# A four-layer graph and feed-forward kernel: making the feed-forward weights in the first stage, spreading the last close over the first slots, and adding the last constant by DMA

## The chip, the cores and the metric

The kernel runs on one core of one Trainium2 chip. The metric is the device time of one launch in microseconds; the time before is the median of three runs. A profile is of one further execution on the chip.

## The reference, cut to what matters

Two layers work on x (4096 rows of 256 columns) and on a sparse integer matrix adj (4096 by 4096). Layer 0 is a graph attention and a feed-forward loop, layer 1 two chained graph attentions and a mixture of experts. Each adds to x.

```python
# layer 0
h = einsum('nd,mdo->mno', layernorm(x), W)                 # 4 heads of 64
e = leaky_relu(f_src[:, :, None] + f_dst[:, None, :], 0.2) # f = h . a1, h . a2
x = x + elu(softmax(where(adj > 0, e, -9e15)) @ h)         # heads side by side
y = layernorm(x)
for _ in range(30):                                        # the feed-forward loop
    y = y + 0.01 * tanh(y)
    y = y * sigmoid(y)
    y = layernorm(y, ln_w, ln_b) @ W_ffn.T + b
x = x + y
# layer 1
x = x + gat(gat(layernorm(x)))      # two attentions as above
x = x + experts(layernorm(x))       # router, top 2 of 6, three matmuls each
```

## The kernel before, in words

One core runs five stages one after the other: attention g0, the feed-forward loop, attentions g1 and g2, the experts. Rows come in 32 tiles of 128; a group is 4 tiles (512 rows), so there are 8 groups. DRAM buffers lie between stages: x1d after g0, x2d after the feed-forward, h1d and x3d after g1 and g2.

**An attention stage** (`attention`) has a first part, its preparation, and a main loop. The preparation goes over the 8 groups: it transposes rows on PE, multiplies them by the head weights, and writes `vals`, two fp16 parts of every value. Small matmuls of all kinds share one PSUM tile there, `small_ps`. In g0 the weights of g0, g1 and g2 are made in it too (list `late`), and the mask pieces are begun: adj comes in 64 loads of 1 MB (`load_piece`, two buffers), VectorE makes a byte pair of each (`make_piece`, L214), a DMA transposes it.

The main loop has 128 units: 4 chunks of 8 row tiles, by 4 heads, by 8 slices q of the columns. Per unit, ScalarE and VectorE make sign tiles `st` (L461, L459), VectorE ANDs the mask in (L567) and XORs the rest (`below`, L573), and PE does 64 fp8 by fp16 matmuls into the accumulators `acc` (L519). After eight units a head is closed: ScalarE scales the low half out of PSUM (`lower_sums`, L468, tile `lo`), VectorE adds (`whole_sums`, L472, tile `u`), which frees the accumulators, and the generator `close` does the rest one step per unit: scale by r, add, add hs, reciprocal and scale, exp into tile `e` (L497), and `finish`, which makes `e` the result (L622, L623) and stores it by the SP queue (L624). `u`, `e` and `old` have one buffer each, `lo` has two. A manual schedule keeps the program's order on VectorE and ScalarE in this loop; the other queues, SP's among them, are ordered by the framework's scheduler. The last head is closed after the loop, all at once.

**The feed-forward stage** first loads its weight by the ScalarE queue, normalizes and scales it through a chain of small operations on PE, VectorE and POOL (L703 to L772), and measures the first groups of x1d. Then it runs 240 slots (30 steps by 8 groups) and six more to drain. A slot issues work of several ages, `slot(at)`:

```python
u = at - 3   # PE transposes z; at end ScalarE copies zT (L846), POOL makes z_rs (L850, L851)
u = at - 5   # VectorE: y = po * rstd + bias, or + last in the last step (L803)
u = at - 2   # ScalarE silu (L815), fp16 parts (L817, L818), SP transposes them (L822)
u = at       # ScalarE tanh (L826), POOL adds (L827); VectorE statistics of u = at - 2
rate(at + 2); init(at + 1); measure(at + 3)   # only in the first eight slots
u = at - 4   # PE: 20 matmuls (L863, L866)
u = at - 5   # last step only: POOL adds y to x1 (L877), SP stores x2d (L878)
```

`measure` takes statistics of a group of x1d on VectorE (L676, L678), `rate` makes the factor and shift x_rs and x_nm on ScalarE and POOL (L684 to L688), `init` applies them on ScalarE into y (L695). All four engines keep the program's order here. The rows of the last four groups of x1d that the end adds are loaded into own tiles (L790), the other four by the stream of row tiles (L92).

Of the kernel before, what the change touches and what calls it, by code (L numbers as in the profile page):

```python
# [11 lines left out]
F32 = mybir.dt.float32  # L12
BF16 = mybir.dt.bfloat16
F16 = mybir.dt.float16
# [32 lines left out]
def gnn_ffn_kernel(ctx: ExitStack, tc: tile.TileContext, a: dict, out: bass.AP):  # L47
# [19 lines left out]
    ones = const.tile([2 * H, P], F32, name="ones")  # L67
    nc.gpsimd.memset(ones, 1.0)
# [10 lines left out]
    x1d = dram.tile([N, C], F32, name="x1d")  # L79
    x2d = dram.tile([N, C], F32, name="x2d")  # L80
# [7 lines left out]
    stream = []  # L88

    def load_ahead(src, g, view=rows_of, queue=nc.sync):  # L90
        t = stream[-1].tile([P, G, C], F32, name="rows")
        queue.dma_start(t, view(src, g))  # L92
        ahead[g] = t

# [32 lines left out]
    def weights(tag, W, a_src, a_dst, norm):  # L127
# [4 lines left out]
        def load(pool):  # L132
            for k in range(KC):
                nc.scalar.dma_start(
                    w[:, k, :C].rearrange("p (h o) -> p h o", h=H),
                    W[:, k * P : (k + 1) * P, :].rearrange("h p o -> p h o"),
                )
            ab = pool.tile([P, 2, H, D], F32, name=f"{tag}_ab")
            nc.scalar.dma_start(ab[:, 0], bcast_rows(a_src))
            nc.scalar.dma_start(ab[:, 1], bcast_rows(a_dst))  # L140
            return ab

        def make(pool, small_ps, ab):
            prod = pool.tile([P, 2, H, D], F32, name="prod")
# [16 lines left out]
    def attention(tag, src, norm, w, others, chunks, first, ends, following):  # L161
# [7 lines left out]
        with ExitStack() as scope:  # L169
            lay = scope.enter_context(tc.tile_pool(name=f"{tag}_lay", bufs=1))  # L170
            vals = lay.tile([P, NT, H, 2, 2, DV], F16, name="vals")
            r = lay.tile([P, NT, H], F32, name="r")
            nf2 = lay.tile([P, NT, H], F32, name="nf2")
            hs = lay.tile([P, 1, H, DV], F32, name="hs")
            mask = [scope.enter_context(tc.tile_pool(name=f"{tag}_mask", bufs=4))]
# [20 lines left out]
            def load_piece(n):  # L196
# [3 lines left out]
                arow[n] = stream[-1].tile([P, 2, 8 * P], I32, name="adj")  # L200
# [32 lines left out]
            with ExitStack() as ps:  # L233
# [44 lines left out]
                def greatest():  # L278
# [8 lines left out]
                    nc.vector.tensor_scalar(dm, ident[: 2 * H, : 2 * H], fx, None, op0=OP.mult)  # L287
                    pt = small_ps()
                    nc.tensor.matmul(pt[:, : 2 * H], ones, dm, start=True, stop=True)
# [107 lines left out]
                late = [functools.partial(make, prep, small_ps, get(prep)) for get, make in others]  # L397
                for g in range(NG + 2):
# [19 lines left out]
                    if g in (3, 5) and late:  # L418
                        late.pop(0)()
                nc.vector.tensor_tensor(r, fs[:, :, :H], mb.to_broadcast([P, NT, H]), OP.add)  # L420
# [17 lines left out]
            end = scope.enter_context(tc.tile_pool(name=f"{tag}_end", bufs=1))  # L438
# [37 lines left out]
            def close(c, h, u):  # L476
# [19 lines left out]
                e = end.tile([P, CM, D], F32, name="e")  # L496
# [40 lines left out]
            with tc.manual_schedule(engines={mybir.EngineType.DVE, mybir.EngineType.Activation}):  # L537
# [3 lines left out]
                for at in range(len(units) + LAG):  # L541
# [43 lines left out]
                    if first:  # L585
# [8 lines left out]
                        if at == len(units) - 30:  # L594
                            store_mask(len(chunks) * PER // 4 - 1)
                    if following and at == len(units) - 2 * following[0]:
# [6 lines left out]
            for _ in close(c, h, u):  # L603
                pass

    def to_rows(dst, src=None):
# [5 lines left out]
        def begin(t, n, h, work):  # L612
            if src is not None:
                old = work.tile([P, 8, D], F32, name="old")
# [20 lines left out]
    with tc.tile_pool(name="adj", bufs=2) as adjacency:  # L635
        stream.append(adjacency)
        attention("g0", x, True, w0, [make, *makers], [8, 8, 8, 8], True, to_rows(x1d, x), [])
    stream.append(ctx.enter_context(tc.tile_pool(name="stream", bufs=4)))

    with ExitStack() as scope:
        one = scope.enter_context(tc.tile_pool(name="f_one", bufs=1))
        wT = one.tile([P, C], F32, name="wT")  # L650
        w16 = one.tile([P, 2, C], F16, name="w16")
        scale = one.tile([P, 2], F32, name="scale")
        under = one.tile([P, 2, G], F32, name="under")
        eps = one.tile([P, 2], F32, name="eps")
        nc.gpsimd.memset(eps[:, :1], EPS)
        nc.gpsimd.memset(eps[:, 1:], EPS * 1e-4)
        bias = one.tile([P, C], F32, name="bias")
        last = one.tile([P, C], F32, name="last")
# [4 lines left out]
        x1 = {}  # L663

        def load(g, queue=nc.sync):
            if g not in ahead:
                load_ahead(x1d, g, queue=queue)
            x1[g] = ahead.pop(g)

        measured, rates = {}, {}  # L670

        def measure(g):
            st = small.tile([P, G, 6], F32, name="x_st")
            mv = measured[g] = small.tile([P, G, 2], F32, name="x_mv")
            for r in range(G):
                nc.vector.bn_stats(st[:, r, :], x1[g][:, r, :])  # L676
            for r in range(G):
                nc.vector.bn_aggr(mv[:, r, :], st[:, r, :])  # L678

        def rate(g):  # L680

            mv = measured.pop(g)
            rs = small.tile([P, G], F32, name="x_rs")
            nc.scalar.activation(rs, mv[:, :, 1], AF.Identity, scale=1e-4, bias=eps[:, 1:])  # L684
            nc.gpsimd.tensor_tensor(rs, rs, mhalf, OP.pow)
            nm = small.tile([P, G], F32, name="x_nm")
            nc.gpsimd.tensor_tensor(nm, mv[:, :, 0], rs, OP.mult)
            nc.gpsimd.tensor_scalar(nm, nm, -1.0, None, op0=OP.mult)  # L688
            rates[g] = rs, nm

        def init(g):
            t = x1.pop(g)
            rs, nm = rates.pop(g)
            for r in range(G):
                nc.scalar.activation(  # L695
                    y[:, g * G + r, :], t[:, r, :], AF.Identity, scale=rs[:, r : r + 1], bias=nm[:, r : r + 1]
                )

        for g in range(4):
            load(g, nc.gpsimd)  # L700
        with tc.tile_pool(name="f_prep", bufs=1) as prep, tc.tile_pool(name="f_pps", bufs=1, space=PSUM) as pps:
            ln = prep.tile([2 * KC, P], F32, name="ln")
            nc.scalar.dma_start(ln[:KC], a["L0_ffn_ln_w"].rearrange("(k p) -> k p", p=P))  # L703
            nc.scalar.dma_start(ln[KC:], a["L0_ffn_ln_b"].rearrange("(k p) -> k p", p=P))
            wr = prep.tile([P, KC, C], F32, name="wr")
            nc.scalar.dma_start(wr, a["L0_ffn_W"].rearrange("(k p) c -> p k c", p=P))
            nc.scalar.dma_start(bias, bcast_rows(a["L0_ffn_b"]))
            for g in range(3):
                measure(g)
                if g < 2:  # L710
                    rate(g)
            init(0)
            ps = pps.tile([P, 2 * KC], F32, name="ps_ln")
            nc.tensor.transpose(ps, ln, ident[: 2 * KC, : 2 * KC])
            lnT = prep.tile([P, 2 * KC], F32, name="lnT")
            nc.vector.tensor_scalar(lnT, ps, 100.0, None, op0=OP.mult)
            lbb = prep.tile([P, KC, P], F32, name="lbb")
            nc.vector.tensor_copy(lbb, lnT[:, KC:, None].to_broadcast([P, KC, P]))
# [661 lines left out]
```

## Time and profile before

| | |
|---|---|
| median of 3 runs | 3016.61 us (3013.63 to 3020.14) |
| the profiled execution, own time | 3008.46 us |
| its span | 3006.8 us |
| mean granted TensorE clock | 0.974 |
| g0, preparation, to its first L519 matmul | 0 to 95.6 us |
| g0, main loop, to its last L519 matmul | 95.6 to 598.4 us |
| first tanh of the feed-forward; its POOL sum in slot 8 | 608.6 us; 652.4 us |
| last tanh of the feed-forward; last POOL sum into x2d | 1553.4 us; 1583.4 us |
| first L519 matmul of g1 | 1644.3 us |

A line of a timeline reads: start in microseconds from the span's start, length, engine, source line, operation, tile written and tiles read, sizes, count, and in brackets the idle time before it and what ended it. `SPq` and `ACTq` are DMAs issued by those queues; the length is then that of the issue. A DMA's landing is not in that line; it is taken from the trace's records of landings, at the sixteenth and last of its parts.

### The profile page before, as it was taken

What the parts mean: (1) busy time and instruction counts of PE and PEld (TensorE: products, weight loads), DVE (VectorE), ACT (ScalarE), POOL (GpSimd) and SP (SyncE); (2) the same over time, 40 slices, a digit from 0 to 9 for tenths busy, and PEclk for the clock granted to TensorE, in tenths of its full rate; (3) what the DMA queues carried; (4) which work ended last, traced back from release to release, by engine and by line L of the source; (5) the groups of instructions that cost most, each with busy time, mean ns of one, the idle gap of its engine ahead of it and who ended that gap; (6) DMA issues with size and microseconds to landing.
All of it is one profiled execution on the core that took longest, in us unless ns stands there. A gap on an engine that the chain in (4) does not pass through costs nothing. (4 is left out here: it accounts for less than half of the span.)

```text
span 3006.8 us, 82646 instructions
## 1 busy us (share of the span) xinstructions
PE 2813.1 (94%) x33923; PEld 2568.3 (85%) x33923; DVE 2741.0 (91%) x5766; ACT 2462.0 (82%) x3132; POOL 1173.2 (39%) x1056
## 2 busy tenths in 40 slices
PE   6899999979999999999998999999889999986996
PEld 5799999958888888888876999999789999975996
DVE  8999999989999999999998899999689999986775
ACT  5799999788888888888866999999699999963442
POOL 2000000089999999999993000000200000013663
PEclk9999999989999999999999999999999999997998
DMA  9999784143333333333343031220303132133253
GB/s 292 267 256 249 224 247 118 33 133 70 68 68 67 68 70 69 68 68 68 68 95 121 20 103 51 76 79 27 107 20 93 51 107 79 51 96 123 82 172 134
DMA packets 482899, 320.08 MB, mean 106 GB/s; under 512 B 416573, under 2 KB 443354, under 8 KB 476378
## 3 DMA queue, kind: packets, MB, share of 16 engines
q1 hardware_dynamic: 467698, 287.13, 35.6%
q0 software_dynamic: 7680, 21.51, 2.3%
q10 hardware_dynamic: 7144, 6.16, 0.6%
q8 instruction: 268, 4.39, 0.6%
q14 instruction: 109, 0.89, 0.1%
HBM read 183.00 MB, written 52.04 MB: 78 GB/s over the span
## 5 line engine op out<-in xcount | busy, mean ns | idle before, releaser
L519 PE MATMUL acc<-vals,st 128*128 128x130 f16 x12288 | 1431.1, 218 | 36.1 <-DVE u L472 27.9
L519 PE MATMUL acc<-vals,below 128*128 128x130 f16 x12288 | 1430.7, 221 | 12.6 <-DVE below L573 11.9
L461 ACT ACTIVATE st<-f1b,nf 128x1024 int8<-128x1024 f32 x1265 | 1334.2, 1142 | 29.9 <-PE acc L519 24.6
L519 PEld LDWEIGHTS <-below 128*128 128x128 fp8e4 x12288 | 1175.7, 96 | 49.4 <-issue 44.5
L519 PEld LDWEIGHTS <-st 128*128 128x128 fp8e4 x12288 | 1207.5, 98 | 9.6 <-DVE st L567 7.5
L863 PE MATMUL po<-wT,zT 128*128 128x256 f32 x1920 | 576.1, 382 | 7.4 <-ACT zT L846 7.4
L827 POOL TENSOR_TENSOR th<-th,y 128x1024 f32<-128x1024 f32 x240 | 568.2, 2368 | 27.2 <-ACT th L826 4.4
L866 PE MATMUL po<-w,zT 128*128 128x256 f16 x3840 | 577.9, 273 | 0.3 <-DMA zT<-z 0.3
L866 PEld LDWEIGHTS <-zT 128*128 128x128 f16 x3840 | 376.3, 98 | 161.6 <-DMA zT<-z 1.2
L573 DVE TENSOR_TENSOR below<-m,st 128x1024 int32<-128x1024 int32 x384 | 470.0, 1224 | 32.8 <-DVE st L567 1.3
L567 DVE TENSOR_TENSOR st<-st,m 128x1024 int32<-128x1024 int32 x384 | 467.5, 1217 | 0.2
L803 DVE SCALAR_TENSOR_TENSOR y<-po,z_rs,bias 128x256 f32<-128x256 f32 x928 | 384.4, 477 | 2.1 <-PE tp L796 0.7
L839 DVE BATCH_NORM_STATS2 z_st<-z 128x6 f32<-128x256 f32 x960 | 335.8, 413 | 0.0
L863 PEld LDWEIGHTS po<-wT,zT 128*128 128x128 f32 x1920 | 291.1, 192 | 17.4 <-ACT zT L846 9.0
L105 POOL TENSOR_TENSOR ln_rstd<-ln_rstd,mhalf 128x4 f32<-128x4 f32 x24 | 32.3, 1345 | 586.5 <-ACT acc L1033 491.8
L815 ACT ACTIVATE z<-th 128x1024 f32<-128x1024 f32 x240 | 251.2, 1047 | 8.6 <-POOL th L827 8.3
L826 ACT ACTIVATE th<-y 128x1024 f32<-128x1024 f32 x240 | 249.8, 1041 | 0.1
L850 POOL TENSOR_TENSOR z_rs<-z_rs,mhalf 128x4 f32<-128x4 f32 x240 | 245.7, 1024 | 0.0
L846 ACT COPY zT<-tp 128x512 f32<-128x512 f32 x240 | 140.4, 585 | 110.5 <-PE tp L796 110.4
L459 DVE TENSOR_SCALAR st<-f1b,nf 128x1024 int8<-128x1024 f32 x271 | 201.2, 743 | 8.4 <-PE acc L519 8.4
L436 POOL MEMSET hs<- 128x4 f32 x3 | 0.3, 101 | 491.9 <-DVE u L489 491.9
L818 DVE SCALAR_TENSOR_TENSOR z<-z,scale,z 128x512 f16<-128x512 f32 x240 | 179.4, 747 | 4.9 <-ACT z L817 4.9
(252 smaller groups left out, 2970.2 us busy)
## 6 DMA issues: line engine op xcount, KB each, us to landing
adj<-in_adj_dram SPq DMA_DIRECT2D x64, 1024.0 KB
m<-edges SPq DMA_DIRECT2D x32, 1024.0 KB
f1b<-fd SPq DMA_DIRECT2D x48, 512.0 KB
edges<-m SPq DMA_DIRECT2D x16, 1024.0 KB
y<-yd SPq DMA_DIRECT2D x16, 512.0 KB
ew<-in_L_ffn_expert_w_dram SPq DMA_DIRECT2D x18, 256.0 KB
t<-in_x_dram SPq DMA_DIRECT2D x8, 512.0 KB
old<-in_x_dram SPq DMA_DIRECT2D x16, 256.0 KB
```

Source lines behind the costliest of these rows:

```text
L461: nc.scalar.activation(out, f1, AF.Sign, bias=f2, scale=-1.0)
L519: nc.tensor.matmul(acc[:, i, cols], masked[part][:, at_i // TR, s, rows], v[:, cols], start=(j == 0 and part == 0), stop=(j == NT - 1 and ...
L567: nc.vector.tensor_tensor(above, above, whole, OP.bitwise_and)
L573: nc.vector.tensor_tensor(below, whole, above, OP.bitwise_xor)
L803: nc.vector.scalar_tensor_tensor(y[:, g * G + r, :], po[:, r, :], rstd[:, r : r + 1], last if end else bias, op0=OP.mult, op1=OP.add,)
L815: nc.scalar.activation(z, th.pop(u), AF.Silu, scale=0.01)
L826: nc.scalar.activation(th[at], y[:, g * G : (g + 1) * G, :], AF.Tanh, scale=0.01)
L827: ins = nc.gpsimd.tensor_tensor(th[at], th[at], y[:, g * G : (g + 1) * G, :], OP.add)
L839: nc.vector.bn_stats(st[:, r, :], z[:, r, :])
L850: nc.gpsimd.tensor_tensor(rs[u], rs[u], mhalf, OP.pow)
L863: nc.tensor.matmul(po[:, r, :], src[:, r * P : (r + 1) * P], wT, start=True, stop=False)
L866: nc.tensor.matmul(po[:, r, :], src16[:, part * G + r, :], w16[:, other, :], start=False, stop=(part == 1 and other == 1),)
```

## The change

Each part is in the diff below, which is cut to what the prediction speaks of.

- The feed-forward weight is loaded and made in g0's preparation (`load_ffn`, `make_ffn`, fourth of the list `late`, at g == 7). Some steps go from VectorE to ScalarE or POOL.
- One persistent `ring` of four row tiles replaces the two adj buffers and the stream of row tiles; `e` becomes the other half of `u`; `old` shares the two buffers of `lo`; the preparation's temporary tiles lie in `u` and `lo` (`spots`). This holds for all three attentions.
- In g0's last 28 units, `side` issues the loads of four groups of x1d, six `add_last`, two `measure`, two `rate` and two `init`. `add_last(g)` copies a group of x1d to x1e in DRAM by SP and adds `last` to it by an accumulating DMA of POOL, for groups 0 to 5.
- The last close of g0 becomes the generator `outro`: its first step follows the loop, the others are in slots 0, 2 and 3. Groups 6 and 7 are loaded after it.
- In the first eight slots `init(at)` stands ahead of the tanh of the same slot, `rate(at + 1)` behind POOL's sum, and both work in place on the loaded rows.
- In the last step, groups 0 to 5 add x1e on VectorE (`po * rstd + x1e`) and need no POOL sum; groups 6 and 7 keep it, now right behind VectorE's.
- In the experts, `numbers` makes its long table in four parts.

```diff
-    def load_ahead(src, g, view=rows_of, queue=nc.sync):
-        t = stream[-1].tile([P, G, C], F32, name="rows")
+    ring = keep.tile([P, 4, G, C], F32, name="ring")
+    def load_ahead(src, g, view=rows_of, queue=nc.sync):
+        t = ring[:, turns[0] % 4]
...
-                arow[n] = stream[-1].tile([P, 2, 8 * P], I32, name="adj")
+                arow[n] = ring[:, 2 * (n % 2) : 2 * (n % 2) + 2].rearrange("p s r c -> p s (r c)").bitcast(I32)
...
-                e = end.tile([P, CM, D], F32, name="e")
+                e = u[:, :, 1, :D]
...
-                old = work.tile([P, 8, D], F32, name="old")
+                old = work.tile([P, 4, 2, DV], F32, name="old", tag="lo", bufs=2)
...
-                    if g in (3, 5) and late:
+                    if g in (3, 5, 7) and late:
                         late.pop(0)()
...
+                    if len(units) - at in side:
+                        side[len(units) - at]()
...
-            for _ in close(c, h, u):
+            closing = close(c, h, u)
+            if tail is not None:
+                next(closing)
+                return closing
+            for _ in closing:
                 pass
...
+    def add_last(g):
+        ins = nc.sync.dma_start(rows_of(x1e, g), rows_of(x1d, g))
+        tc.add_manual_dep(ins.ins, arrived[0].ins.name,
...
+        nc.gpsimd.dma_start(rows_of(x1e, g), last[:, None, :].to_broadcast([P, G, C]), accum_op=OP.add)
...
+    SUMMED = 6
+    side = {
+        28: [(load, g) for g in range(4)],
+        **{24 - 3 * g: [(add_last, g)] for g in range(SUMMED)},
+        8: [(measure, 0)],
+        5: [(measure, 1)],
+        4: [(rate, 0)],
+        2: [(rate, 1)],
+        1: [(init, 0), (init, 1)],
+    }
...
+                t = x1.pop(g) if end else None
+                summed = end and g < SUMMED
                 for r in range(G):
                     nc.vector.scalar_tensor_tensor(
-                        y[:, g * G + r, :],
+                        t[:, r, :] if summed else y[:, g * G + r, :],
                         po[:, r, :],
                         rstd[:, r : r + 1],
-                        last if end else bias,
+                        t[:, r, :] if summed else last if end else bias,
...
+                if end and not summed:
+                    nc.gpsimd.tensor_tensor(t, t, y[:, g * G : (g + 1) * G, :], OP.add)
+                if end:
+                    nc.sync.dma_start(rows_of(x2d, g), t)
...
-                nc.scalar.activation(th[at], y[:, g * G : (g + 1) * G, :], AF.Tanh, scale=0.01)
+                if 2 <= at < NG:
+                    init(at)
+                was = x1.pop(at) if at < NG else y[:, g * G : (g + 1) * G, :]
+                nc.scalar.activation(th[at], was, AF.Tanh, scale=0.01)
...
-            if at + 2 < NG:
-                rate(at + 2)
-            if at + 1 < NG:
-                init(at + 1)
-            if at + 3 < NG:
-                measure(at + 3)
+            if 2 <= at + 1 < NG:
+                rate(at + 1)
+            if at == 0:
+                next(outro)
+                measure(3)
+            if at == 2:
+                next(outro)
...
+            if at == 3:
+                for _ in outro:
+                    pass
+                for g in range(SUMMED, NG):
+                    load_apart(x1d, g)
+            if 4 <= at + 2 < NG:
+                measure(at + 2)
...
-            u = at - 5
-            if units - NG <= u < units:
-                g = u % NG
-                t = x1.pop(g)
-                nc.gpsimd.tensor_tensor(t, t, y[:, g * G : (g + 1) * G, :], OP.add)
-                nc.sync.dma_start(rows_of(x2d, g), t)
```

## The prediction

> **What bounds the kernel now.** I read the page's busy times first, then the stretches by stage, then the timelines of the three places that the change touches: the head boundaries of the attentions, the first slots of the feed-forward and its last ones.
>
> ```profile
> PE 2813.1 (94%) x33923; PEld 2568.3 (85%) x33923; DVE 2741.0 (91%) x5766; ACT 2462.0 (82%) x3132; POOL 1173.2 (39%) x1056
> ```
>
> PE and VectorE are both nearly full over the span, so there is little free cover on VectorE. The stretches (busy time and count of PE, weight loads, VectorE, ScalarE, POOL) are g0's main loop, the feed-forward's start, its steady part:
>
> ```profile
> 95.60:598.20 502.60, 480.21 (x8192) 475.28 (x8192) 483.52 (x532) 475.16 (x479) 3.77 (x4) 0.99 0.71 197
> 598.20:652.40 54.20, 31.04 (x162) 22.09 (x160) 44.03 (x145) 44.42 (x78) 38.98 (x46) 0.75 0.55 158
> 652.40:1553.40 901.00, 901.00 (x6439) 737.87 (x6437) 898.86 (x2992) 783.58 (x1154) 863.04 (x691) 1.00 0.35 68
> ```
>
> In the main loop a unit takes 3.69 us of PE, and the loss is at head boundaries: in chunks 0 to 2 PE waits 0.7 to 3.2 us ahead of a head's first matmul, in chunk 3, g1 and g2 0.5 us in its middle. What ends it is the sum that frees the accumulators. From the list of who waited for L472, in us and times:
>
> ```profile
>   PE acc L519: 27.9, 45
> ```
>
> The feed-forward's start has all engines part idle: 54 us for what becomes 3.9 us a slot. Between slots 3 and 7 the tanh comes every 5.47 us, and POOL is what is full. Slot 4 of the POOL timeline:
>
> ```profile
> 632.56 2.37 POOL L827 TENSOR_TENSOR th<-th,y 128x1024 f32<-128x1024 f32 x1
> 634.88 1.04 POOL L850 TENSOR_TENSOR z_rs<-z_rs,mhalf 128x4 f32<-128x4 f32 x1
> 636.00 0.20 POOL L851 TENSOR_TENSOR z_rs<-z_rs,under 128x4 f32<-128x4 f32 x1
> 636.15 1.01 POOL L685 TENSOR_TENSOR x_rs<-x_rs,mhalf 128x4 f32<-128x4 f32 x1
> 637.24 0.51 POOL L687 TENSOR_TENSOR x_nm<-x_mv,x_rs 128x4 f32<-128x4 f32 x1
> 637.84 0.23 POOL L688 TENSOR_SCALAR x_nm<-x_nm 128x4 f32<-128x4 f32 x1
> 638.03 2.36 POOL L827 TENSOR_TENSOR th<-th,y 128x1024 f32<-128x1024 f32 x1
> ```
>
> From one th sum to the next POOL never rests; x_nm is ready 5.5 us after the sum began. ScalarE's init, which uses such an x_nm one slot later, and tanh:
>
> ```profile
> 633.14 2.06 ACT L695 ACTIVATE y<-rows,x_nm,x_rs 128x256 f32<-128x256 f32 x4
> ...
> 636.82 1.04 ACT L826 ACTIVATE th<-y 128x1024 f32<-128x1024 f32 x1
> ```
>
> At the end, POOL's sums into x1 push its th sums apart, 6.3 us where 3.92 is the pace:
>
> ```profile
> 1553.00 2.37 POOL L877 TENSOR_TENSOR rows<-rows,y 128x1024 f32<-128x1024 f32 x1
> 1555.33 2.35 POOL L827 TENSOR_TENSOR th<-th,y 128x1024 f32<-128x1024 f32 x1
> ...
> 1559.33 2.37 POOL L877 TENSOR_TENSOR rows<-rows,y 128x1024 f32<-128x1024 f32 x1
> 1561.65 2.80 POOL L827 TENSOR_TENSOR th<-th,y 128x1024 f32<-128x1024 f32 x1
> ```
>
> [...] The trace agrees where DMA is quiet (g1's head stores land 2.55 us after issue) and shows up to 5.2 where it is not. [...] the one at 616.23 shows 1.28 us and no drain, so I use 1.28. [...] a VectorE multiply of 128x1 took 2.29 us (616.10) beside POOL's sum; L687 varies from 0.19 to 0.62.
>
> **The change part by part.**
>
> (a) *Weight in g0's preparation.* From 28 us on VectorE is back to back there, and it sets when the main loop begins. It gains (rows of 602 to 621 us) lnT 0.15, bias 0.42, two subtractions 0.75, two reductions 0.83, nine small ones at some 0.12, wT 0.38, w16's second part 0.45: 4.0 us. In the built order the last of these stand between the sign tiles and the first `below`, and wait for POOL's power (0.58) and ScalarE's w16 (0.35); pieces and values of the last group stand around the earlier waits. I add 0.5: **+4.5** (2 to 6.5; the low end if VectorE's gaps, 0.2 to 0.5 us each, take half). The loads go by ScalarE's queue at 0.25 to 0.5 us an issue, beside work. The first stage's PE and ScalarE additions lie in their gaps. Moving the weight frees nothing at 602 to 621 by itself; that is counted in (e).
>
> (b) *e in u.* New wait: the first sum of a head (L472) writes u, so it must wait for the store of the head before, which reads u. In the built order this sum now has a DMA semaphore among its waits, at all 45 boundaries; before, it waited for ScalarE alone. SP and VectorE at one boundary:
>
> ```profile
> 563.64 0.36 SPq L624 DMA_DIRECT2D x1d<-e  x1
> ```
>
> ```profile
> 567.32 0.69 DVE L472 TENSOR_TENSOR u<-acc,lo 128x520 f32<-128x520 f32 x1
> ```
>
> The sum starts 3.68 us after the store's issue, the store lands 4.86 after it: 1.18 us short. The same subtraction at every boundary gives, where positive, in g0's chunks 0 to 2 0.92, 1.61, 0.45, 0.01, 0.46, 0.29, around chunk 3 0.07, 0.82, 1.18, in g1 1.39, 0.74, 1.33, 0.74, in g2 1.05, 0.72, 1.44. Behind that sum stand VectorE's AND and XOR, and PE waits for the accumulators. In chunks 0 to 2 PE already waits for exactly this, so it adds in full: 3.7. Elsewhere the present stall of 0.5 takes the first half microsecond: 0.3 + 2.2 + 1.7 (the 1.18 goes under (d)). Sum **+8** (2 to 14: the high end adds all shortfalls in full and something for the wait itself).
>
> (c) *Copies and accumulating DMAs.* SP isn't under the manual order. In the built order the copies of groups 0 and 1 stand ahead of the store of the head before last of chunk 2, and wait for the first load of x1d; those of 4 and 5 wait for the next store. So at the boundary into chunk 3, two 512 KB copies are in front of a store that had 4.2 us. No DRAM-to-DRAM copy is in the trace; a 512 KB load lands in 3.7 to 4.5 us[...]. POOL's six accumulating DMAs run beside it; POOL itself is idle (4 instructions in the loop). I take **+4** (0 to 7) at this one boundary.
>
> (d) *measure in the last units.* Two of 1.73 us (1.37 + 0.36) go into VectorE's order at 8 and 5 units from the end, where VectorE's `below` is 0.8 to 2.0 us ahead of PE. The first delays a head's sum by 1.7, less the present 0.5: 1.2; with the third measure spread over the last units the lead is used up, 1.3 more: **+2.5** (0.5 to 4). init of two groups, 4.1 us, falls into ScalarE's idle 8.6 us at 588 to 596: nothing.
>
> (e) *First slots.* Keep the last matmul at 598.4. ScalarE has lo by 599.1 and goes to tanh at once: POOL's first th sum at 600.2, not 609.7, and slot 2 no longer waits for the weight. But init(at) now stands ahead of tanh(at), and rate(at + 1) behind the th sum of slot at on POOL. That closes a ring: th sum, z_rs, rate on POOL 5.5 us, then init 2.06, tanh 1.04 and two hand-overs of 0.07, then the next th sum: 8.75 us a slot, where 5.47 was. Step by step, slot 2 sums at 609.9; exp between two silus costs two more table loads (2.6), so slot 3 sums at 618.2; then 626.95, 635.7, 644.45, 653.2, and slot 8 at 656.95 (3.75 later). Before, slot 8 summed at 652.4. So 9.5 us early becomes **+4.5** late (1 to 7: L687 at its 0.2 or 0.6 in each turn[...]). What is late next is y of slot 5, which waits for nothing else.
>
> (f) *Last slots.* Six of eight POOL sums of 2.36 go, and SP no longer holds transposes behind x2d stores that wait for POOL. At a pace of 3.92 from 1546.75 the last y begins at 1574 and ends at 1575.3, not 1581.7; PE is free at 1573.5, not 1579.2. g1's preparation follows PE and these rows: **-6** (-8 to -4).
>
> The ring, `lo` for `old`, and the split table (iotas and casts of POOL, some 4 us at 2694 to 2699, read from 2727 on) I cost at nothing: the rows' buffers alternate as before, and 28 us cover the table. Without that cover the table costs at most 2.
>
> Sum: 4.5 + 8 + 4 + 2.5 + 4.5 - 6 = **+17.5**, on the profiled execution's 3008.46. That one lies 8.2 under the median; against 3016.6 I forecast **3034**.
>
> **Rivals.** *Faster*, 0.11: POOL does rate in the shadow of ScalarE and the ring of (e) does not bind. Then slots 4 to 8 keep 5.47, (e) is -8.5, and with (a), (b) and (c) at their low ends, 2, 2 and 0, the sum is -8: 3009. It decides at a turn under some 6.5 us. For it: the work is the same and two inits fewer. Against: POOL's program order. *No change*, 0.12: stores land in time, (b) and (c) vanish into existing stalls; 4.5 + 2.5 + 4.5 - 6 = 5.5, 3022, or less. For it: g1's quiet landings of 2.55. *Worse*, 0.14: the copies and accumulating DMAs slow all of chunk 3's stores by 3 us or more, and (b) reaches its high end: +31, 3048. That the change doesn't do what it says is not among them: the built order shows each piece in place.
>
> **How the numbers follow.** The forecast has 0.63. About 0.2% (6 us) is what a measurement of this kernel can tell from no change. Slower holds the forecast and the worse case, 0.77; the same 0.12; faster 0.11. The parts' ends, half of each added in squares, give about 9 us either way for the forecast; to leave no more than 2 in 10 out with the no-change and worse cases, the range is 3012 to 3047.
>
> **What would show it.** In the changed profile: L472's successor idle for a DMA of x1d, h1d and x3d; PE's first L519 near 100; the boundary into chunk 3 worst; tanh of slots 4 to 7 some 8.7 us apart; th sums evenly 3.92 apart to the end. Tanh steps of 5.5, or a u sum that starts as early as before, would make it wrong.

## The result, and the profile after

The changed kernel has a median of 3028.91 us (3026.85 to 3038.2); the kernel before, run beside it, 3018.47 (3013.63 to 3026.25). The ratio is 1.0038 [1.0026, 1.005], some 11.5 us more. In a later comparison it was 1.0026 [1.0016, 1.0037]. The kernel before takes 3006 to 3024 us from one chip to another, so only ratios to runs beside it are compared. The two profiled executions are 21 us apart (own times 3008.46 and 3029.54), more than the medians: that pair misleads, and the table takes each kernel twice.

| stretch, us | before, two profiles | after, two profiles | difference of means | predicted |
|---|---|---|---|---|
| start to first matmul of the main loop | 95.6, 95.1 | 103.2, 103.5 | +8.0 | +4.5 (a) |
| g0's main loop | 502.8, 506.1 | 509.1, 510.7 | +5.5 | +10.5 (b, c, d) |
| its end to the th sum of slot 8 | 54.0, 54.0 | 59.4, 59.5 | +5.5 | +4.5 (e) |
| slots 8 to 200 | 751.8, 751.8 | 752.2, 753.6 | +1.1 | 0 |
| slots 200 to 239 | 157.5, 157.5 | 153.0, 153.0 | -4.5 | with the next |
| last th sum to g1's first matmul | 82.7, 81.5 | 77.4, 77.6 | -4.6 | -6 with the one above (f) |
| g1's main loop | 486.8, 485.6 | 488.0, 487.9 | +1.8 | +2.2 (b) |
| g2's preparation | 64.9, 65.2 | 54.3, 53.2 | -11.3 | 0 |
| g2's main loop | 485.7, 486.4 | 488.8, 490.1 | +3.4 | +1.7 (b) |
| last stage | 325.1, 323.0 | 342.5, 326.6 | not repeated | 0 |

The last stage's code differs in the table of `numbers` and in where its rows lie. Rows one to nine add up to +4.9; the forecast had +17.5 for them, and the -11.3 not at all. The last stage's 342.5 did not come back in the second profile. Between +4.9 and the measured 7.8 to 11.5 lie 3 to 7 us that the last stage and the spread between executions may hold; they are not settled.

The page's busy times after:

```profile
PE 2812.7 (93%) x33923; PEld 2566.3 (85%) x33923; DVE 2733.1 (90%) x5756; ACT 2467.5 (81%) x3139; POOL 1177.9 (39%) x1061
```

No engine's work changed by more than 8 us over the span: what was added is mostly waiting. The stretches of g0's main loop, the feed-forward's first slots and its steady part (busy time and count of PE, weight loads, VectorE, ScalarE, POOL; then the PE clock, DMA share and GB/s):

```profile
103.20:612.10 508.90, 483.00 (x8192) 477.98 (x8192) 484.44 (x537) 480.28 (x490) 17.65 (x14) 0.99 0.77 207
612.10:671.70 59.60, 27.13 (x145) 19.56 (x143) 36.93 (x121) 43.34 (x69) 35.70 (x38) 0.77 0.44 115
671.70:1572.90 901.20, 901.06 (x6437) 737.68 (x6436) 898.88 (x2991) 783.29 (x1154) 863.48 (x691) 1.00 0.39 69
```

In the first slots there is less to do, since the weight is made elsewhere, and yet more idle time: VectorE is busy for 37 of 59.6 us, where it was for 44 of 54.2. The loop grew with its PE work unchanged. Who ended VectorE's idle time ahead of the sum into u (us, times), and how long PE waited for that sum:

```profile
  DMA h1d<-u: 11.0, 4
  DMA x1d<-u: 5.7, 3
  DMA x3d<-u: 5.5, 3
...
  PE acc L534: 35.1, 46
```

The stores of x1d, h1d and x3d now hold the sum up, as (b) said, and PE's wait for it went from 27.9 to 35.1. (The last line is of the list of who waited for the sum.) In the first slots, slot 5 on POOL, then the ScalarE steps of slot 6:

```profile
651.20 2.35 POOL L894 TENSOR_TENSOR th<-th,x 128x1024 f32<-128x1024 f32 x1 [3.28 <-ACT th L893]
653.50 1.04 POOL L917 TENSOR_TENSOR z_rs<-z_rs,mhalf 128x4 f32<-128x4 f32 x1
...
656.14 0.23 POOL L770 TENSOR_SCALAR x_nm<-x_nm 128x4 f32<-128x4 f32 x1
659.65 2.35 POOL L894 TENSOR_TENSOR th<-th,x 128x1024 f32<-128x1024 f32 x1 [3.28 <-ACT th L893]
```

```profile
656.40 2.07 ACT L776 ACTIVATE x<-x,x_nm,x_rs 128x256 f32<-128x256 f32 x4 [2.73 <-POOL x_nm L770]
658.51 1.06 ACT L893 ACTIVATE th<-x 128x1024 f32<-128x1024 f32 x1
```

This is the ring of (e): 2.73 us of ScalarE waiting for POOL, then 3.28 of POOL waiting for ScalarE, 8.45 us a turn. And the last slots, where the sums of 6.3 us spacing were:

```profile
1565.01 2.37 POOL L894 TENSOR_TENSOR th<-th,y 128x1024 f32<-128x1024 f32 x1
...
1568.93 2.36 POOL L894 TENSOR_TENSOR th<-th,y 128x1024 f32<-128x1024 f32 x1
```

They keep 3.92 almost to the end. The shortfall that nobody looked for is at g2's start. ScalarE's first copy out of the transposes, and PE from there, in the kernel before:

```profile
2141.82 0.60 ACT L274 ACTIVATE xT<-tp 128x512 f32<-128x512 f32 x1 [5.24 <-DMA h1d<-e]
```

```profile
2132.80 1.09 PE L113 MATMUL tp<-ident,rows 128*128 128x128 f32 x8 [1.43 <-DVE u L472]
2142.57 5.92 PE L300 MATMUL ph<-g_w,xT 128*128 128x264 f32 x16 [8.67 <-ACT xT L274]
```

and after the change:

```profile
2145.03 0.60 ACT L278 ACTIVATE xT<-tp 128x512 f32<-128x512 f32 x1 [1.92 <-PE tp L114]
```

```profile
2143.90 1.09 PE L114 MATMUL tp<-ident,ring 128*128 128x128 f32 x8 [1.43 <-DVE u L487]
2145.77 3.83 PE L304 MATMUL ph<-g_w,xT 128*128 128x264 f32 x16 [0.78 <-ACT xT L278]
```

The copy reads transposes of the first group, which were there at 2133.9, but before the change it waited for the store of the last head of g1, a DMA that has nothing to do with its data. A writer that waits for a reader of another tile most likely shares its memory: xT of g2's preparation would lie where `e` of g1 had lain. No view shows addresses; the run end first, below, tests it. Then 16 matmuls took 5.92 us in place of 3.83. The change creates the pool `end` (u, lo, z) at the head of the attention instead of after the preparation:

```diff
+            end = (tail or scope).enter_context(tc.tile_pool(name=f"{tag}_end", bufs=1))
...
-            end = scope.enter_context(tc.tile_pool(name=f"{tag}_end", bufs=1))
```

These lines were in the diff that the prediction was made from, and it gave them no step.

### The profile page after: what moved, and what is told of

It reads as the page before. It is cut to its first block, busy times and chain, and to the rows that moved or that the text cites. A ratio compares the mean times of both kernels' runs of the same rounds, so it can differ in the third digit from the quotient of the medians.

```text
span 3027.8 us, 82647 instructions
## 1 busy us (share of the span) xinstructions
PE 2812.7 (93%) x33923; PEld 2566.3 (85%) x33923; DVE 2733.1 (90%) x5756; ACT 2467.5 (81%) x3139; POOL 1177.9 (39%) x1061
## 5 line engine op out<-in xcount | busy, mean ns | idle before, releaser
L534 PE MATMUL acc<-vals,st 128*128 128x130 f16 x12288 | 1433.8, 219 | 40.2 <-DVE u L487 35.1
L894 POOL TENSOR_TENSOR th<-th,y 128x1024 f32<-128x1024 f32 x232 | 548.6, 2365 | 19.8
L893 ACT ACTIVATE th<-y 128x1024 f32<-128x1024 f32 x232 | 241.7, 1042 | 0.0
```

The source lines that it names most:

```text
L534: nc.tensor.matmul(acc[:, i, cols], masked[part][:, at_i // TR, s, rows], v[:, cols], start=(j == 0 and part == 0), stop=(j == NT - 1 and ...
L893: nc.scalar.activation(th[at], was, AF.Tanh, scale=0.01)
L894: ins = nc.gpsimd.tensor_tensor(th[at], th[at], was, OP.add)
```

## The experiments

Each ran beside the kernel before on one chip. "First", "loop", "ramp" are the first, second and third rows of the table above. An attention has 16 heads in its main loop; a head's length is the time from its first matmul to that of the next.

**The kernel before, again.** No edit.

> The kernel before, unchanged, profiled a second time. The profile after is 21 us longer than the profile before, but the medians are only 10.4 us apart; of the 21, 17.4 arise in the last stage (from g2's last matmul to the end), which the change does not touch, and -10.6 in g2's preparation, which it does not touch either. Theory A: these two are spread between executions. Then a second profile of the kernel before shows the last stage (325.1 us in the first profile) or g2's preparation (64.8) different by 5 us or more, while g0's and the feed-forward's moments (first matmul of the main loop 95.6, end of g0 598.4, slot 8's sum 652.4) stay within 1 us. Theory B: the change causes them, through addresses or order. Then the second profile repeats 325.1 and 64.8 within 2 us. The ratio to itself should be 1.000 within 0.003.

Ratio 1.0003 [0.9994, 1.0011]. g2's preparation repeats (65.2), so its shortening belongs to the change: theory B for that stage. The last stage repeats too (323.0), so this run alone would give its 342.5 to the change as well; the second profile of the changed kernel, below, decides that. The loop did not repeat within the microsecond expected: 506.1 against 502.8, with three heads 0.6 to 1.6 us longer.

**rate first.**

```diff
+            if 2 <= at + 1 < NG:
+                rate(at + 1)
             if at < units:            # tanh and th sum of slot at
...
-            if 2 <= at + 1 < NG:
-                rate(at + 1)
```

> The changed kernel, with rate(at + 1) put ahead of the tanh and th sum of slot at instead of behind z_rs; everything else as changed. Theory A (ring): the tanh of slots 4 to 7 comes every 8.3 to 9.3 us because POOL's order closes a ring th sum, z_rs, rate, init, tanh. With rate ahead of the th sum, init no longer waits for the sum of the slot before; the turn falls to what POOL has to do, 5.5 us, slot 8 sums at some 59.4 - 5 x 3 = 45 us after g0's last matmul (54.0 in the kernel before), and the run gains 12 to 15 us against the changed kernel: ratio to the kernel before 0.998 to 1.000. Theory B: ScalarE, VectorE's measures[...] set the turn. Then it stays above 7.5 us and the gain is under 5 us (ratio 1.002 to 1.004).

Ratio 1.0002 [0.9993, 1.001]: the ramp is 50.8 instead of 59.4, 8.6 us, with everything else unmoved. POOL from slot 6 of this kernel on, and ScalarE for slot 7:

```profile
654.68 2.36 POOL L896 TENSOR_TENSOR th<-th,x 128x1024 f32<-128x1024 f32 x1
657.00 1.04 POOL L919 TENSOR_TENSOR z_rs<-z_rs,mhalf 128x4 f32<-128x4 f32 x1
658.12 0.25 POOL L920 TENSOR_TENSOR z_rs<-z_rs,under 128x4 f32<-128x4 f32 x1
660.03 2.37 POOL L896 TENSOR_TENSOR th<-th,x 128x1024 f32<-128x1024 f32 x1 [1.67 <-ACT th L895]
```

```profile
656.81 2.06 ACT L776 ACTIVATE x<-x,x_nm,x_rs 128x256 f32<-128x256 f32 x4
658.90 1.06 ACT L895 ACTIVATE th<-x 128x1024 f32<-128x1024 f32 x1
```

init has no wait ahead of it, and a turn takes 5.35 us. The ring was POOL's program order, theory A, with the ratio just above its band; the gain of 8.6 is under the 12 to 15 expected, because the steps up to slot 3 and one of 8.7 us between slots 4 and 5 stayed.

**No copies.**

```diff
-        **{24 - 3 * g: [(add_last, g)] for g in range(SUMMED)},
...
-                load_ahead(x1e, g)
+                load_ahead(x1d, g)
...
-                load_apart(x1e if g < SUMMED else x1d, g)
+                load_apart(x1d, g)
```

> The changed kernel without the six copies from x1d to x1e and the six accumulating DMAs; the feed-forward's last slots read x1d, so the constant of the last layer is left out of these six groups. Theory A, as predicted: the copies delay the head stores and with them the sums around the boundary into chunk 3; then end of g0 moves 4 us (0 to 7) earlier than in the changed kernel, between heads 22 and 28 of 32. Theory B, from the profile after: the boundary is only 1.4 us longer there, and what remains in chunk 3 comes from the wait of u on every store and from the measures; then g0 ends 0.5 to 2 us earlier and the ratio to the kernel before stays 1.003 to 1.004.

Ratio 1.0019 [1.0012, 1.0026]. The head before the boundary into chunk 3 is 32.79 us again, the kernel before's length; with the copies it is 33.8 to 34.3. The next and the fifteenth head stay long (31.09 and 31.40, before 29.49 and 29.98). So the copies cost 1.0 to 1.5 us at one boundary, as theory B has it, though the ratio is below its 1.003. (The place that the expectation names is this boundary.) They cost it only together with the wait of `u`: in the run e in w the copies are there, and this head is 32.78. This kernel leaves out the constant of six groups.

**No weight.**

```diff
-        [make, *makers, (load_ffn, make_ffn)],
+        [make, *makers],
...
+    for t, v in ((wT, 0.0), (w16, 0.0), (scale, 1.0), (under, 1.0), (bias, 0.0), (last, 0.0)):
+        nc.gpsimd.memset(t, v)
```

> The changed kernel with the making of the feed-forward's weight left out: weight, bias, last and scales are constants from memsets, so the values of all later stages differ, and the last stage, which routes by values, is not comparable. Theory A, as predicted: VectorE's own instructions and their waits are what the weight costs in g0's preparation, 4.5 us (2 to 6.5) of it; the first matmul of the main loop comes back from 103.2 to 97 to 99. Theory B: all of the 7.6 us seen is the weight; the first matmul comes at 95.6 within 0.7. Theory C: part comes from the other moves in this preparation (the making of the other weights in u and lo, the ring for the pieces), and 1 us or more of the 7.6 stays.

Ratio 1.0017 [1.001, 1.0025]. First is 96.6. In the seven profiles with the whole weight it is 101.9 to 103.5, mean 102.8; in the five that start as the kernel before does, 94.5 to 97.6, mean 95.5. By these means the weight is 6.2 of 7.3 us. The value lies between the bands of A and B, and at the edge of C, since 1.0 us of the 7.6 stays; but the kernel before itself varies by 3.1 us here, so that this rest is not shown to be a cost. What is settled is that A's 4.5 is too little.

**The changed kernel, again.** No edit.

> The changed kernel, unchanged, profiled a second time. Its first profile has a last stage of 342.5 us, where the kernel before has 325.1 and 323.0 and three variants of the changed kernel 325.9 to 331.3. Theory A: that length belongs to that execution and chip, not to the change. Then the last stage is 323 to 329 us here, the moments up to it stay within 3 us of the first profile (first matmul 103.2, end of g0 612.3, slot 8 59.4 after it, g2's preparation 54.2), and the ratio to the kernel before is 1.002 to 1.004. Theory B: the change lengthens the last stage by 10 us or more; then it is above 335 again and the ratio above 1.004.

Ratio 1.0026 [1.0016, 1.0037]; the last stage is 326.6 us. Theory A. In the two comparisons where the kernel before had a median of 3018 and 3024 the changed kernels' last stages were 342.5 and 343.8, in the others, beside 3006 to 3008, 322 to 331 with either code. So it is most likely the chip that makes this stage longer, and the first profile before stands 8 us under its median for the same reason. That is argued and not shown.

**end first.** The kernel before, with its pool moved for g1 and g2.

```diff
+            if not first:
+                end = scope.enter_context(tc.tile_pool(name=f"{tag}_end", bufs=1))
             mask = [scope.enter_context(tc.tile_pool(name=f"{tag}_mask", bufs=4))]
...
-            end = scope.enter_context(tc.tile_pool(name=f"{tag}_end", bufs=1))
+            if first:
+                end = scope.enter_context(tc.tile_pool(name=f"{tag}_end", bufs=1))
```

> The kernel before with one edit: in g1 and g2 the pool end (u, lo, e, z) is allocated ahead of the mask's, as in the changed kernel, instead of after the preparation. Theory A: g2's preparation is 11.2 us shorter in all four profiles of the changed kernel because its xT lies where g1's e lay before; ScalarE's copy waited 5.3 us for the landing of the last head's store, PE idled 8.7 us and its granted clock fell to 0.50, so the next 16 matmuls took 6.85 us, not 3.83. With end in its own place this goes: g2's preparation 53 to 55 us instead of 65, ratio 0.996 to 0.9975. Theory B: the ring of rows buffers or another of the change's moves did it; then g2's preparation stays at 64 to 66 and the ratio at 1.000.

Ratio 0.9977 [0.9969, 0.9984], and g2's preparation 56.0 us. ScalarE's first copy, then PE:

```profile
2130.63 0.60 ACT L276 ACTIVATE xT<-tp 128x512 f32<-128x512 f32 x1 [1.92 <-PE tp L113]
```

```profile
2131.37 5.52 PE L302 MATMUL ph<-g_w,xT 128*128 128x264 f32 x16 [0.78 <-ACT xT L276]
```

The wait on the store is gone: theory A, though 56.0 and 0.9977 are a little short of its bands. This one line explains 9 of the 11.3 us, and 10 in the run both of these, which has the same edit and takes 55.0. The difference from the changed kernel is in the matmuls, 5.52 us for 3.83: the granted clock is 0.57 here from 2131 to 2135, where the changed kernel has 1.00 from 2144 to 2152. In the profile before, PE is idle from 2133.9 to 2142.6 and the clock is 0.50 from 2138 to 2146. Why it is low here, where PE idled 1.43 and 0.78 as in the changed kernel, stays open.

**The last slots alone.** The kernel before with the sums into x1e (as in the change's diff) and

```diff
+            g, rest = divmod(at - 40, 8)
+            if 0 <= g < SUMMED and rest == 0:
+                nc.sync.dma_start(rows_of(x1e, g), rows_of(x1d, g))
+            if 0 <= g < SUMMED and rest == 4:
+                nc.gpsimd.dma_start(rows_of(x1e, g), last[:, None, :].to_broadcast([P, G, C]), accum_op=OP.add)
```

> The kernel before with the last slots' part of the change alone: six groups of x1d are copied to x1e and get the last constant by accumulating DMAs, here in the feed-forward's steady slots 40 to 84 (a copy every 8 slots, its accumulating DMA 4 slots later), and the last sums go into these rows. Theory A: the part is worth what the profiles show from slot 8 to g1's first matmul, 991.9 and 990.7 us before, 982.6 in the changed kernel: 8.5 us less, of which DMA issues on POOL in the full steady part take back 0 to 4. Ratio 0.997 to 0.9985. Theory B: the copies disturb the steady part's transposes or POOL's pace and give it all back: ratio 0.9985 to 1.001.

Ratio 1.003 [1.0019, 1.0042]: longer by more than theory B allowed. The last slots are 153.0 and what follows 78.1, 8.5 us less, as theory A has it; but slots 40 to 100 take 254.4 us where they took 235.2. (SP is ordered by the scheduler, and the copies themselves went at 257 to 507 us, in g0's loop.) POOL at the first accumulating DMA:

```profile
790.36 1.39 POOL L798 DMA_DIRECT2D x1e<-last  x1
791.24 2.91 POOL L843 TENSOR_TENSOR th<-th,y 128x1024 f32<-128x1024 f32 x1
793.56 2.02 POOL L866 TENSOR_TENSOR z_rs<-z_rs,mhalf 128x4 f32<-128x4 f32 x1
```

The issue takes 0.9 us of an engine that has none to spare, and throws POOL and VectorE out of step: the sum is 2.91 instead of 2.37, the power 2.02 instead of 1.03. Four slots take 4.66, 4.57, 4.02 and 4.02 us instead of 3.92; in all six places these make 9.4 us. Beside that SP's queue holds the load of the same rows until that DMA has landed, 6.2 to 6.7 us, with transposes behind it, and PE waits for a transpose once in each place, here in the last:

```profile
974.32 1.04 PE L882 MATMUL po<-w,zT 128*128 128x256 f16 x4 [5.58 <-DMA zT<-z]
```

So the fifth slot takes 0.0 to 6.2 us more, 9.8 in all six. The two together are the 19.2 us. In the changed kernel the accumulating DMAs stand in g0's loop, where POOL is busy for 17.65 of 508.9 us, and slots 40 to 100 take 235.2: that place is what makes (f) a gain.

**Both of these.** The two edits above together.

> The kernel before with both edits: end ahead of the mask in g1 and g2, and the last slots' part with its copies in slots 40 to 84. If the two are independent, as theory A of each has it, the gains add: 11.2 + 5 to 8.5, ratio 0.9935 to 0.9955, and this is the shortest of all kernels here. If theory B of one holds, only the other's gain is left.

Ratio 1.0012 [1.0005, 1.0018]: g2's preparation 55.0, last slots 153.0 and 78.1, slots 40 to 100 254.4. The parts add, with the loss among them: neither theory's 0.9955 or less, and not the shortest.

**e in w.** `e` gets memory of its own again.

```diff
-                e = u[:, :, 1, :D]
+                e = w.rearrange("p k c -> p (k c)")[:, : CM * D].rearrange("p (i d) -> p i d", d=D)
```

> The changed kernel with e in memory of its own: in the attention's own weight w, which nothing reads after the preparation, instead of in the second half of u. The first sum of a head then waits for no store. Theory A, as predicted, the wait of u costs 8 us: 4.0 in g0's loop, 2.2 in g1, 1.7 in g2. From the profiles of the two kernels (before: loop 502.5 to 506.1, g1 485.3 to 486.8, g2 485.6 to 486.4; changed: 509.1 to 510.7, 487.8 to 488.0, 488.8 to 490.1): g1 comes back to 486, g2 to 486, the loop by 2 to 4 to 506 or 507; ratio to the kernel before 0.9995 to 1.001. Theory B: the wait hides and the longer loop is the copies' and the measures' alone; then loop, g1 and g2 stay within 0.7 us of the changed kernel and the ratio at 1.0026. g2's preparation stays short (53 to 55) in both, since w lies apart from the preparation's own tiles.

Ratio 1.0008 [0.9999, 1.0016]. g1 is 486.3, g2 485.3, the loop 508.2; the heads ahead of chunk 1 and at the start of chunk 3 are 30.51 and 29.49, exactly the first profile before. Of what ended VectorE's idle time ahead of that sum, and who waited for it:

```profile
  ACT lo L483: 46.6, 59
...
  PE acc L534: 28.9, 44
```

No DMA is left, and PE's wait is back at 28.9. Theory A, but for the loop, which was to be 506 or 507: its first head took 37.71 us. A stage's first head varies from profile to profile with either place of `e`, in g0 from 33.6 to 37.7, so the wait of `u` is better read from the other fifteen:

| fifteen heads, us | `e` in memory of its own | `e` in u | difference of means |
|---|---|---|---|
| g0, changed kernel | 470.5, 471.8 | 474.1 to 475.5 (5 profiles) | 3.7 |
| g1 | 449.8 to 449.9 (7) | 451.7 to 452.5 (7) | 2.0 |
| g2 | 449.8 to 449.9 (7) | 451.1 to 454.9 (7) | 2.8 |

The row of g0 has only kernels with the copies and the early measures in the loop. Together the wait is worth 8.4 us, and the copies' 1.0 to 1.5 are among them: the head ahead of chunk 3 is 32.78 here, though the copies run.

**Both repairs.** rate first, and e in w.

> The changed kernel with both edits: rate ahead of the th sum, and e in w. If the ring and the wait of u are the two independent costs that the steps have them to be, their gains add: 8.6 us in the first slots and 5 to 9 in the three attentions, ratio to the kernel before 0.996 to 0.9985, below 1.000 for certain. If the wait of u hides, the ratio stays at 1.000 as with rate first alone.

Ratio 0.9967 [0.9955, 0.9979], median 2996.65 against 3008.17: the shortest of all, some 10 us under the kernel before. Ramp 50.9, g1 486.4, g2 485.5, loop 507.7. Both gains are there whole, so the two costs are independent.

**Measures late.**

```diff
-        8: [(measure, 0)],
-        5: [(measure, 1)],
-        4: [(rate, 0)],
-        2: [(rate, 1)],
-        1: [(init, 0), (init, 1)],
+        0: [(measure, 0), (measure, 1), (rate, 0), (rate, 1), (init, 0), (init, 1)],
```

> The changed kernel with measure, rate and init of groups 0 and 1 put behind the last unit of g0's loop instead of into its last eight units. Theory A, as predicted: the two measures of 1.73 us delay VectorE's below and with it PE, 2.5 us (0.5 to 4): the loop's last two heads come back by 1.4 to 2.5 us, but the first tanh, which comes 0.9 us after g0's last matmul in the changed kernel, waits for measure, rate and init, some 7 to 9 us, and the run is 5 to 8 us longer than the changed kernel, ratio 1.004 to 1.0055. Theory B: the last heads are longer for the wait of u alone; then they stay as they are, and the run is 7 to 9 us longer.

Ratio 1.0029 [1.0017, 1.0042], no longer than the changed kernel. The fifteenth head goes from 31.40 to 29.98, the kernel before's length, so theory A has the cause and 1.4 us the size. Most of what I expected to be lost was not: the first th sum comes 4.3 us after the loop, against 1.7, since VectorE runs ahead of PE and is through with the two measures at 610.2, before PE's last matmul at 612.5. Slot 8 is 2.4 us later, counted from the loop's end, and that head 1.4 shorter.

**Loads only.**

```diff
-        [make, *makers, (load_ffn, make_ffn)],
+        [make, *makers, (load_ffn, make_nothing)],
```

> The changed kernel with the weight's loads in g0's preparation kept (0.4 MB by ScalarE's queue) and the making left out: the raw weight and bias stand in the tiles, scales are constants, w16 zero, so the values of all later stages differ. The first matmul of the main loop comes at 102.7 to 103.5 with loads and making, at 96.6 without both. Theory A: the making on VectorE and PE is the cost, as the prediction sums it; then the first matmul comes at 96 to 98 here. Theory B: this preparation is bound by DMA (its share is 0.9 to 1.0 in both kernels) and the added loads hold up the pieces of the adjacency, 0.4 MB at 290 GB/s being 1.4 us or more; then it comes at 98.5 to 102. Ratios to the kernel before: A 1.001 to 1.002, B 1.002 to 1.003.

Ratio 1.0017 [1.0007, 1.0027]; first is 98.8. What VectorE waited for ahead of the mask's pairs and ahead of `fs`, until the first matmul, before, in this kernel, and after (the last figure of each, us):

```profile
L214 DVE TENSOR_SCALAR pair<-adj 128x2048 int8<-128x2048 int32 x12 | 14.7, 1226 | 0.7 <-DMA adj<-in_adj_dram 0.7
L314 DVE TENSOR_TENSOR fs<-ph,ln_rstd 128x16 f32<-128x16 f32 x16 | 2.5, 163 | 1.2 <-PE ph L300 1.2
```

```profile
L218 DVE TENSOR_SCALAR pair<-ring 128x2048 int8<-128x2048 int32 x12 | 14.7, 1224 | 2.3 <-DMA ring<-in_adj_dram 2.3
L318 DVE TENSOR_TENSOR fs<-ph,ln_rstd 128x16 f32<-128x16 f32 x16 | 2.6, 162 | 2.3 <-PE ph L304 2.3
```

```profile
L218 DVE TENSOR_SCALAR pair<-ring 128x2048 int8<-128x2048 int32 x12 | 14.7, 1226 | 3.1 <-DMA ring<-in_adj_dram 3.1
L318 DVE TENSOR_TENSOR fs<-ph,ln_rstd 128x16 f32<-128x16 f32 x16 | 2.6, 161 | 3.2 <-PE ph L304 3.2
```

98.8 lies in theory B's band, the ratio in theory A's. By the means, of 7.3 us 1.1 belong to neither (96.6 less 95.5), 2.2 come with the loads (98.8 less 96.6) and 4.0 with the making (102.8 less 98.8). The loads' share rests on one profile each of two kernels, and the five profiles that start as the kernel before does spread over 3.1 us; that VectorE's wait for adj grows, from 0.0 to 0.7 in those five to 1.5 to 3.5 in the seven with the whole weight, agrees with it but doesn't settle its size.

Nor does the making end with the first matmul. In the changed kernel the first matmul starts at 103.22, and VectorE has these instructions of the weight ahead of the first `below`, for which PE then waits:

```profile
103.26 0.15 DVE L724 TENSOR_SCALAR big<-far 128x1 f32<-128x1 f32 x1
...
104.39 0.48 DVE L741 SCALAR_TENSOR_TENSOR w<-u,scale,w 128x256 f16<-128x256 f32 x1
104.80 1.22 DVE L588 TENSOR_TENSOR below<-m,st 128x1024 int32<-128x1024 int32 x1
```

```profile
106.11 0.27 PE L534 MATMUL acc<-vals,below 128*128 128x130 f16 x1 [2.50 <-DVE below L588]
```

g0's first head takes 34.2 to 37.7 us with the making, mean 35.6, and 33.6 to 34.4 in the five profiles and the two without it. Up to the end of this head the whole of (a) is 138.3 less 129.5, 8.8 us: 0.9 that is not shown to be a cost, 2.2 with the loads, 5.7 with the making.

## Why the prediction was right, and where its steps were not

The direction was right and 3028.9 is in the range, but the forecast of +17.5 stands against +11.5 [7.8, 15.1] and +7.8 [4.8, 11.1]. One step was missing, worth -11.3, and the others came to about +16, with errors either way. So that 3028.9 came near 3034 is partly luck: (a) was 4.3 too small where (c), (d) and (f) together were some 7 too high, and 3 to 7 us of the measured difference lie in no stage that both profiles repeat. Beside the later chip's 3007 the changed kernel took 3015.5.

- **Missing: the pool `end`.** Its move was in the diff and had no step. The sign that it would matter was in the profile before: ScalarE's 5.24 us behind a store of other rows. end first shows it.
- **(a) +4.5; 8.8 up to the end of g0's first head.** VectorE's own 4.0 was sized right: its busy time up to the first matmul went from 79.7 to 82.0 us, and some 1.6 more lie between it and the first `below`. The failed terms are the 0.5 for waits, where the making cost 5.7, so 1.7 beyond VectorE's work, and "the loads go by ScalarE's queue ..., beside work". Of the five issues, 0.25 to 2.46 us each, two stand ahead of ScalarE's first work, a table load that starts at 18.75 where it started at 15.43. Nor do the bytes seem to be beside work: DMA share in this stretch was 0.98 before, at 287 GB/s, and VectorE's wait for adj is 0.7 there before, 2.3 with the loads and 3.1 with all. The size of that part, 2.2, and the rest of 0.9 are open.
- **(b) +8; about 7, and 8.4 with (c) in it.** The mechanism and the sum were right, the split was not. In g0 chunks 0 to 2 were to give 3.7; of their heads only the one ahead of chunk 1 grew, by 0.8 to 1.8, and one profile of the kernel before has 0.6 of that too. The first head of chunk 3 grew instead, to 31.1 or so, a length that one of five profiles of the kernel before also has. g1 gave 2.0 for 2.2; g2 gave 1.2 to 5.0, 2.8 in the mean, for 1.7. The landings of one execution bound such a sum, but place it badly.
- **(c) +4; 1.0 to 1.5.** The place and the mechanism were right: the copies hold up a store, and the sum waits for that store. In the profile after, the first two copies, issued at 480.69 and 481.37, land 5.96 and 6.64 us later, and the store issued behind them at 482.88 lands 6.13 us after its issue; the same head's store took 3.18 before. The 4 was the author's estimate, made without a trace of such a copy, and too large, as its low end allowed.
- **(d) +2.5; 1.4.** The measure is seen at the fifteenth head alone; the second term, 1.3 for a used-up lead, did not appear.
- **(e) +4.5; +5.5, and 1.1 until slot 40.** Turns of 8.45 for 8.75. The two table loads of ScalarE came where they were expected, around exp at 624.81 and 626.74 of the profile after, with 1.28 us each, as the one at 616.23 before had. rate first shows the order on POOL as the cause. The rival Faster needed a turn under 6.5; rate first has that turn, and its first slots are 8.6 shorter.
- **(f) -6; -9.1.** Half of it lies ahead of the last sum and half behind: what follows the last sum also shrank, by 4.6. The last slots alone repeats both halves, 4.5 and 4.0.
- **The ring, `old` in `lo`, the split table: nothing seen, as forecast.** But for the two long ones the last stage is 323 to 329 us with the table before and 322 to 327 with the split one, 331 where the weight's values are left out. The ring and `old` have no run of their own.

The worst case of all stores late did not occur. That the no-change case was near is due to the missing step, not to stores landing in time. For the landing of a head's store what counts is this trace: eleven of g1's sixteen stores of 256 KB before took 2.54 to 2.57 us, four 5.17 to 5.23, and the last 3.92.

## What to carry to other kernels

When a diff moves the creation of a pool, list which tiles then share memory with which, and look in the profile before for instructions that wait on a DMA of data that they don't use: that is memory handed on, and moving one line was worth 9 us here, as much as the rewritten last slots. A small producer behind a large operation on an engine that keeps the program's order can close a ring when its consumer moves one step closer, as rate and init did here; moving the producer ahead of the large operation cuts it (a turn went from 8.45 us to 5.35). Memory that a store still reads is not free memory, which was 8.4 us here: look for a tile that is dead in the loop, like the weight here.

## What the runs showed of the hardware that I had not expected

- An accumulating DMA of 512 KB took 1.3 to 1.9 us to issue on POOL (1.31 to 1.39 in the last slots alone, 1.49 to 1.86 in the profile after) and landed 6.2 to 6.7 us later in the last slots alone, 6.8 to 15.1 in the profile after. With POOL full, its issue of 0.9 us net cost 1.6 us in the four slots that follow the first one.
- The last stage took 322 to 331 us in twelve profiles and 342.5 and 343.8 in two, where the kernel before ran longer too, while g0 to g2 agreed within a few microseconds.
- After a wait of 8.67 us 16 matmuls of 128x264 took 5.92 and, in the second profile before, after 8.74, 6.85 us; after 0.78 they took 3.83 in the changed kernel and 5.52 in end first. The granted clock was 0.50 in the first two (2142 to 2146; 2143 to 2147), 1.00 in the third and 0.57 in the last.
- In the clock records of the first profiles before and after, the granted clock is 0.50 or 1.00, and every stretch of one of them, but for the last of each profile, lasts a whole multiple of 3.41 us: 3.41 to 30.72 at 0.50, among them 10.24 at the start of g2's preparation before, from 2136.58 to 2146.82.
